# Scores and values of the first two key tiles ahead of the mean of x, and a new order of the first loads

## Chip, cores and metric

The kernel runs on one core of one Trainium2 chip. The metric is the device time of one execution in microseconds (us), the median of the runs.

## What is computed

Two layers on x of shape 8 x 64 x 64 x 64 (images, channels, rows, columns); n = 4096 positions. The first is attention with centred queries and keys plus a "unary" term, the second a binarised convolution with a gate. Only the first is touched by the change:

```python
xf = x.reshape(b, cin, n)
q = jnp.einsum('oc,bcn->bon', wq, xf) + bq[None, :, None]
k = jnp.einsum('oc,bcn->bon', wk, xf) + bk[None, :, None]
v = jnp.einsum('oc,bcn->bon', wv, xf) + bv[None, :, None]
q_mean = q.mean(axis=2, keepdims=True)
k_mean = k.mean(axis=2, keepdims=True)
q = q - q_mean
k = k - k_mean
sim = jnp.einsum('bcn,bcm->bnm', q, k) / (scale * TEMPERATURE)   # scale = 8
sim = jax.nn.softmax(sim, axis=2)
out = jnp.einsum('bnm,bcm->bcn', sim, v)
unary = jax.nn.softmax(jnp.einsum('bc,bcm->bm', q_mean[:, :, 0], k), axis=-1)
out_unary = jnp.einsum('bcm,bm->bc', v, unary)
out = out + out_unary[:, :, None]
return x + out.reshape(b, C, h, w)
```

## The kernel before

**Tiles.** Two images of 64 channels fill the 128 partitions: a "pair". There are 4 pairs, each with 8 blocks of 512 queries, and each block runs over 32 tiles of 128 keys. `projection()` (L157) forms mm = wq'wk once, so that scores come straight from x: for tile j, `scores` (L493) multiplies x's 128 key columns by q, where q = mm'x - mx, and mx is mm applied to the mean of x (`mean_scores`, L307, and `mean_scores_out`, L315). Four matmuls of 64 x 512 make the scores of one tile for both images (line L497), ScalarE takes exp with the scale 1/8 (L508), `weighted` (L511) multiplies by the values in four more matmuls (L516), and `summed` adds the exponentials for the denominator (L532, L534). `values(g)` (L329) makes the values of four key tiles at a time in 16 small matmuls with 65 columns: 64 of wv and one, mx + kb, whose exponential weights the unary term; kb = wk'bq comes from `key_bias()` (L162).

**Order.** Nothing is scheduled by a planner: `tc.manual_schedule()` keeps the order in which the program is written, engine by engine[...]. Waits come from the data: a tile that is written or read elsewhere is waited for as a whole, so that two engines that write two halves of one tile (q's halves in `queries_out`, L463) write one after the other. `attend` (L1079) runs over the 32 blocks; `plan(g)` lists, for each of the 32 key tiles of a block, what else is issued there with `put`. For each tile j it issues the scores of j, then the weighted product of j-1, then what the plan holds. In the first block, g = 0, the plan holds `values(i)` at tile 4i-1 (tile 0 for i = 0) and `unary_part(i)` at 4i+1, and at tile 0 `mix`, which makes the queries of block 1 in two matmuls (`pq`, L455) and their copies (L465 on VectorE, L466 on ScalarE).

**The start, which the change touches.** The loads are issued at L85 to L89: on ScalarE's queue wq, the second quarter of x, wv; on SyncE's queue wk and the three other quarters of x; on GpSimd's queue the 21 small vectors `vec`. Then (L1265 to L1286) TensorE gets 6 filler matmuls (`warm`, on a tile of ones; nothing reads the result), the projection, 4 fillers, the queries of block 0 without the mean (`queries`, L454), 18 fillers, the mean's matmul and the bias of keys; VectorE sums x's first and third quarter and half of the fourth (`mean_part`, L291), ScalarE the rest, between which lie `vectors()` (L167: three small VectorE operations on `vec`, a square root and a first exponential on ScalarE, each with a table load); `load_weights()` (L94) issues nine loads of convolution weights on SyncE after a VectorE memset; then `mean_sum`, `mean_scores`, `mean_scores_out`, `queries_out(0)` (the queries minus mx), `key_bias`, `value_weights` (L321), and the blocks begin.

Of the kernel before, what the change touches and what calls it, by code (L numbers as in the profile page):

```python
# [18 lines left out]
F32 = mybir.dt.float32  # L19
BF16 = mybir.dt.bfloat16  # L20
I32 = mybir.dt.int32
AF = mybir.ActivationFunctionType
ALU = mybir.AluOpType
# [3 lines left out]
P = 128  # L27
C = 64
# [3 lines left out]
QB = 512  # L32
NQ = N // QB
NK = N // P
ROWS = QB // HH
SPLIT = [slice(0, 224), slice(224, QB)]
H = C
# [8 lines left out]
def conv_seq_kernel(ctx, tc, x, wq, wk, wv, vecs, w1, w3, w5, wtap, gw, out):  # L46
    nc = tc.nc
    n_pairs = x.shape[0] * x.shape[1] // P
# [21 lines left out]
    def load_x(name, rows, queues=(nc.sync,)):  # L70
        xt = x_tile(name)
        for c in range(4):
            cols = bass.ts(c, N // 4)
            queues[c % len(queues)].dma_start(out=xt[:, cols], in_=xf[rows, cols])
        return xt
# [8 lines left out]
    w_tap = xp.tile([P, FIRST[3], C], F32, tag="v", name="w_tap")  # L84
    nc.scalar.dma_start(out=wq_s, in_=wq)  # L85
    nc.sync.dma_start(out=wk_s, in_=wk)
    nc.gpsimd.dma_start(out=vec, in_=vecs)
    xt = load_x("0", slice(0, P), (nc.sync, nc.scalar, nc.sync, nc.sync))
    nc.scalar.dma_start(out=wv_s, in_=wv)  # L89


# [56 lines left out]
    ngb = cp.tile([P, 1], F32, tag="ngb", name="ngb")  # L148
    inv = cp.tile([P, 3], F32, tag="inv", name="inv")

    def warm(n):

        t = ps_s.tile([P, 2, QB], F32, tag="s", name="warm")[:, 0, :]
        for _ in range(n):
            nc.tensor.matmul(t[:, 0:P], ones, ones, start=True, stop=True)  # L155

# [5 lines left out]
    def key_bias():  # L162
        t = m_tile("kb_p")
        nc.tensor.matmul(t[:, 0:1], wk_s, bq_s, start=True, stop=True)
        nc.vector.tensor_copy(kb, t[:, 0:1])  # L165

    def vectors():  # L167
        nc.vector.tensor_scalar(inv, rv, BN_EPS, None, ALU.add)
        nc.vector.tensor_scalar(bv2, bv_s, 2.0, None, ALU.mult)
        nc.vector.tensor_scalar(ngb, gb_s, -1.0, None, ALU.mult)  # L170
        nc.scalar.activation(inv, inv, AF.Sqrt)

        nc.scalar.activation(lim[:, 2:3], ones[:, 0:1], AF.Exp)
# [103 lines left out]
    class Pair:  # L277
# [40 lines left out]
            self.nmx = self.tile(sm, "nmx", 0, (P, 1))  # L318
            nc.vector.tensor_scalar(self.nmx, self.pm[:, 0:1], -1.0 / N, None, ALU.mult)

        def value_weights(self):  # L321

            self.v = self.tile(xp, "v", 0, (P, NK, P))
            wx = self.wx = self.tile(sm, "wx", 0, (P, C + 1))
            for b in range(2):
                nc.vector.tensor_copy(wx[img[b], 0:C], wv_s[img[b], img[b]])
            nc.vector.tensor_tensor(wx[:, C : C + 1], self.mx, kb, ALU.add)

        def values(self, g, unary=True):  # L329

            pv = ps_s.tile([P, 2, QB], F32, tag="s", name=f"pv_{self.name}_{g}")
            w = C + 1
            for i in range(4):
                for h in range(2):
                    for b in range(2):
                        nc.tensor.matmul(  # L336
                            pv[img[h], b, i * w : (i + 1) * w],
                            self.x[img[b], bass.ds((4 * g + i) * P + h * H, H)],
                            self.wx[img[b], :],
                            start=True,  # L340
                            stop=True,
                        )
            pvv = pv[:, :, 0 : 4 * w].rearrange("p b (t c) -> p b t c", c=w)
            nc.scalar.copy(
                self.v[:, 4 * g : 4 * g + 4, :].rearrange("p t (b c) -> p b t c", b=2),
                pvv[:, :, :, 0:C],
            )
            if unary:
                if g == 0:
                    self.eu = self.tile(sm, "eu", 0, (P, 2, NK))  # L350
                nc.scalar.activation(
                    self.eu[:, :, 4 * g : 4 * g + 4], pvv[:, :, :, C], AF.Exp
                )
# [136 lines left out]
            nc.vector.tensor_scalar(q[:, SPLIT[0]], data[0], self.mx, None, ALU.subtract)  # L490
            nc.scalar.activation(q[:, SPLIT[1]], data[1], AF.Identity, bias=self.nmx)

        def scores(self, qb, j, neg=None):  # L493
            ps = ps_s.tile([P, 2, QB], F32, tag="s", name=f"ps_{self.name}_{qb}_{j}")
            for h in range(2):
                for b in range(2):
                    nc.tensor.matmul(  # L497
                        ps[img[h], b, :],
                        self.x[img[b], bass.ds(j * P + h * H, H)],
                        self.q[qb][img[b], :],  # L500
                        start=True,
                        stop=neg is None,
                    )
            if neg is not None:
                for b in range(2):
                    nc.tensor.matmul(ps[:, b, :], ones[img[b], :], neg[img[b], :], start=False, stop=True)
            e = ep.tile([P, 2, QB], F32, tag="e", name=f"e_{self.name}_{qb}_{j}")
            nc.scalar.activation(e, ps, AF.Exp, scale=1.0 / 8.0)  # L508
            return e
# [559 lines left out]
    def acc_banks(name):  # L1069
        return [ps_a.tile([P, QB], F32, tag=f"acc{h}", name=f"{name}_{h}") for h in range(2)]  # L1070

    def misc_banks(name):
        return [m_tile(f"{name}_{h}") for h in range(2)]
# [2 lines left out]
    def rows_of(pr):  # L1076
        return slice(pr * P, (pr + 1) * P)

    def attend(pairs):  # L1079
        pending = None  # L1080
        n_blocks = n_pairs * NQ

# [6 lines left out]
        def plan(g):  # L1089
# [4 lines left out]
            def put(i, f, *a):  # L1094
                at.setdefault(i, []).append((f, a))
# [66 lines left out]
                    put((15, 12)[qb - 2] + 4 * i, pairs[pr - 1].store, NQ // 2 * (qb - 2) + i, rows_of(pr - 1))  # L1162
            if g == 0:
                for i in range(NQ):
                    put(max(4 * i - 1, 0), pairs[0].values, i)
                    put(4 * i + 1, pairs[0].unary_part, i)
                put(31, pairs[0].unary_sum)
                for i, n in enumerate((2, 1, 0)):
                    put(8 + 8 * i, weight_mean, n)
                    put(12 + 8 * i, weight_scale, n)  # L1170
# [38 lines left out]
        for g in range(n_blocks):  # L1209
            pr, qb = divmod(g, NQ)  # L1210
            at = plan(g)
            p = pairs[pr]
            for j in range(NK):
                new = (p, qb, j, p.scores(qb, j))
                if pending is not None:
                    pending[0].weighted(*pending[1:])
                    pending[0].summed(*pending[1:], g < n_blocks - 1)
                for f, a in at.pop(j, ()):
                    f(*a)
                pending = new  # L1220
            assert not at, at.keys()
# [42 lines left out]
    with tc.manual_schedule():  # L1264
        first = Pair("0", xt)  # L1265
        warm(6)
        projection()
        warm(4)
        first.mean_part(0, quarters[0])
        vectors()  # L1270
        first.mean_part(1, quarters[1], True)
        first.mean_part(2, quarters[2])
        for c in range(2):
            first.mean_part(3 + c, slice(N * (6 + c) // 8, N * (7 + c) // 8), c == 1)
        first.query_tiles(0, score_banks)
        for b in range(2):
            first.queries(0, b)
        load_weights()
        warm(18)
        first.mean_sum(5)  # L1280
        first.mean_scores()
        first.mean_scores_out()
        first.queries_out(0)
        key_bias()
        first.value_weights()
        attend([first] + [None] * (n_pairs - 1))  # L1286


    nb_ = sm.tile([P, 1], F32, tag="nb", name="nb")
# [127 lines left out]
```

## Time and profile before

| | |
|---|---|
| Three runs | 1902.95, 1903.20, 1903.52 us; median 1903.2 |
| Profiled execution, its own time | 1902.88 us |
| Its span, first to last instruction | 1901.1 us |
| TensorE busy / weight loads | 1882.2 us (99%) / 781.2 us (41%) |
| VectorE / ScalarE / GpSimd busy | 1587.3 us (83%) / 1276.6 us (67%) / 129.1 us (7%) |
| Mean granted TensorE clock | 0.997 |
| Scores, L497 | 8192 passes, 0.86 us for each tile's 8 when in full flow |
| First score matmul / first weighted product begin | 12.92 us / 17.15 us |

How to read it. The page gives one profiled execution; times within it count from its first instruction. PE is TensorE's matmuls, PEld its weight loads, DVE is VectorE, ACT ScalarE, POOL GpSimd, SP SyncE. One matmul in the program on 4-byte numbers stands as two in the profile (4 of a tile's scores are 8 there). Rows of the timeline are: start, length, engine, line, operation, what is written <- what is read, shape, count, and in brackets how long the engine stood idle before and what ended that. In tables of stages the columns are the stage, its length, busy time (and instructions) of PE, PEld, DVE, ACT and POOL, the granted TensorE clock, the share of the DMA engines and GB/s. The page names the releaser that came last by its own record; where two engines' results are waited for it can name a neighbour: the wait of ACT L466 is put down to the copy of kb, while the program has it wait for VectorE's half of q just before that.

### The profile page before, as it was taken

To read this page: it belongs to the slowest core of one execution; us is meant where nothing else is said; L and a number is where in the kernel's file an instruction comes from. 1 tells how busy PE (TensorE), PEld (TensorE's weight loads), DVE (VectorE), ACT (ScalarE), POOL (GpSimd) and SP (SyncE) were. 2 spreads that over 40 slices of the span, in tenths; PEclk is the share of its full clock that TensorE was granted. 3 is DMA by queue.
4 is the path that set the end of the run, shared out by engine and by line. 5 is a ranking of instruction groups with operands and counts; after the bars stand their busy time and mean duration, and the time that the engine had idled before them with its cause. 6 is when DMAs were issued, how large, how long until landed. Compare 5 with 4: busy or idle time off the path is not lost.

```text
span 1901.1 us, 50325 instructions
## 1 busy us (share of the span) xinstructions
PE 1882.2 (99%) x21502; PEld 781.2 (41%) x21502; DVE 1587.3 (83%) x2485; ACT 1276.6 (67%) x1639; POOL 129.1 (7%) x177
## 2 busy tenths in 40 slices
PE   9999999999999999999999999999999999999997
PEld 4333344443344434444434444434433344443343
DVE  6779888889888888888888888888887888887876
ACT  5666776666666676666666667666666666666663
POOL 0000000000000000000000000000000000000000
PEclk9999999999999999999999999999999999999998
DMA  4334433333333533333333444233333344333311
GB/s 124 65 60 102 80 68 72 67 58 72 67 71 82 122 81 82 65 72 66 58 71 68 102 112 92 51 79 67 70 67 64 65 84 94 85 72 63 71 35 47
DMA packets 73024, 142.22 MB, mean 75 GB/s; under 512 B 10380, under 2 KB 40920, under 8 KB 72664
## 3 DMA queue, kind: packets, MB, share of 16 engines
q0 software_dynamic: 22352, 81.29, 24.2%
q1 hardware_dynamic: 49720, 56.46, 10.4%
q8 instruction: 170, 2.79, 0.6%
q10 hardware_dynamic: 720, 1.18, 0.2%
q14 instruction: 62, 0.51, 0.1%
HBM read 39.27 MB, written 89.78 MB: 68 GB/s over the span
## 4 chain that ended last, share of the span: by engine, by line
PE 98%; DVE 1%; ACT 1%; DMA 0%; issue 0%; SPq 0%; DVEq 0%; ACTq 0%
PE ps L497 46%; PE acc L516 46%; PE z L804 2%; PE pv L336 1%; PE pq L483 1%; PE z L891 0%; PE z_5e L804 0%; DMA x<-in_x 0%; PE warm L155 0%; ACT e L508 0%; DVE r L609 0%; DVE sb L936 0%; ACT rc_ck L441 0%; DVE o L542 0%; DVE es_j L936 0%
## 5 line engine op out<-in xcount | busy, mean ns | idle before, releaser
L508 ACT ACTIVATE e<-ps 128x1024 f32<-128x1024 f32 x1024 | 1049.0, 1025 | 570.9 <-PE ps L497 557.9
L534 DVE TENSOR_TENSOR es<-es,e 128x1024 f32<-128x1024 f32 x836 | 1020.7, 1221 | 197.3 <-ACT e L508 184.0
L497 PE MATMUL ps<-q,x 64*64 64x512 f32 x8192 | 1084.5, 590 | 0.8 <-DVE kb L165 0.8
L516 PE MATMUL acc<-e,v 64*64 64x512 f32 x8192 | 1082.6, 589 | 2.2 <-ACT e L508 1.9
L516 PEld LDWEIGHTS acc<-e,v 64*64 64x64 f32 x8192 | 324.4, 131 | 558.7 <-ACT e L508 317.6
L497 PEld LDWEIGHTS ps<-q,x 64*64 64x64 f32 x8192 | 344.1, 133 | 493.5 <-issue 266.5
L555 POOL DMA_DIRECT2D es<-e x93 | 80.0, 860 | 902.1 <-ACT e L508 598.7
L871 DVE SCALAR_TENSOR_TENSOR sb<-pt,sb 128x256 f32<-128x256 f32 x174 | 65.9, 420 | 0.0
L804 PEld LDWEIGHTS <-wc 64*64 64x64 bf16 x3364 | 60.1, 106 | 2.7 <-issue 1.0
L555 POOL DMA_DIRECT2D es<-es x31 | 26.6, 857 | 440.3 <-DVE es L534 426.1
L804 PE MATMUL z<-ec,wc 64*64 64x128 bf16 x1392 | 53.6, 217 | 0.0
L532 DVE TENSOR_TENSOR es<-e,e 128x1024 f32<-128x1024 f32 x32 | 39.2, 1224 | 17.0 <-ACT e L508 17.0
L804 PE MATMUL z<-t,wc 64*64 64x128 bf16 x1392 | 53.1, 217 | 0.3 <-DVE o L542 0.3
L652 ACT ACTIVATE s<-x,vec 128x512 bf16<-128x512 f32 (+2 forms) x66 | 46.2, 702 | 7.7 <-DVE x L620 7.7
L834 ACT ACTIVATE pt<-z,frac 128x256 f32<-128x256 f32 (+1 forms) x87 | 41.1, 543 | 8.9 <-PE z L804 8.9
L839 DVE SCALAR_TENSOR_TENSOR pt<-z_5e,frac,pt 128x256 f32<-128x256 f32 x29 | 14.0, 484 | 38.2 <-PE z_5e L804 38.2
L553 POOL DMA_DIRECT2D es<-e x31 | 17.3, 558 | 339.6 <-ACT e L508 328.3
L542 DVE COPY o<-acc 128x512 f32<-128x512 f32 (+2 forms) x33 | 22.2, 675 | 9.6 <-PE acc L516 9.6
L845 DVE TENSOR_TENSOR pt<-pt 128x384 f32<-128x384 f32 x58 | 29.6, 552 | 0.0
L336 PEld LDWEIGHTS pv<-wx,x 64*64 64x64 f32 x1024 | 22.5, 134 | 16.9 <-issue 9.3
L570 DVE TENSOR_TENSOR e_parts<-e_parts 128x512 f32<-128x512 f32 x31 | 21.4, 689 | 6.3 <-DMA e_parts<-es 6.3
L620 DVE SCALAR_TENSOR_TENSOR x<-x,ou,x 128x512 f32<-128x512 f32 (+2 forms) x33 | 24.3, 736 | 1.2
(178 smaller groups left out, 882.6 us busy)
## 6 DMA issues: line engine op xcount, KB each, us to landing
es<-e POOLq DMA_DIRECT2D x124, 512.0 KB, 5.3
es<-es POOLq DMA_DIRECT2D x31, 512.0 KB, 5.4
e_parts<-es SPq DMA_DIRECT2D x124, 128.0 KB, 3.1
r<-rc SPq DMA_DIRECT2D x62, 128.0 KB, 3.0
out<-sb SPq DMA_DIRECT2D x28, 256.0 KB, 3.3
x<-in_x SPq DMA_DIRECT2D x24, 256.0 KB, 3.9
ec<-t SPq DMA_DIRECT2D x29, 99.0 KB, 4.7
xc<-in_x SPq DMA_DIRECT2D x30, 72.0 KB
```

Of the source, the lines that this page charges most:

```text
L336: nc.tensor.matmul(pv[img[h], b, i * w : (i + 1) * w], self.x[img[b], bass.ds((4 * g + i) * P + h * H, H)], self.wx[img[b], :], start=True ...
L497: nc.tensor.matmul(ps[img[h], b, :], self.x[img[b], bass.ds(j * P + h * H, H)], self.q[qb][img[b], :], start=True, stop=neg is None,)
L508: nc.scalar.activation(e, ps, AF.Exp, scale=1.0 / 8.0)
L516: nc.tensor.matmul(self.acc[qb][h][img[b], :], self.v[img[h], j, img[b]], e[img[h], b, :], start=(j == 0), stop=(j == NK - 1),)
L532: nc.vector.tensor_tensor(self.es[qb], self.first, e, ALU.add)
L534: nc.vector.tensor_tensor(self.es[qb], self.es[qb], e, ALU.add)
L555: nc.gpsimd.dma_start(out=out, in_=e, accum_op=ALU.add)
L652: nc.scalar.activation(sy[n][0][:, rows, pad : pad + HH], self.x2[qb][:, r0 * HH : r1 * HH].rearrange("p (h w) -> p h w", w=HH), AF.Sign, ...
L804: nc.tensor.matmul(z[img[b], :].rearrange("p (q w) -> p q w", w=HH), wc[k][img[h], n, c * C : c * C + C], src[:, first : first + step + 1 ...
L834: nc.scalar.activation(out, z, AF.Identity, scale=frac[:, by : by + 1])
L845: nc.vector.tensor_tensor(self.pairs[:, :, :, r, :], t[:, 0:3, 0], t[:, 0:3, 1], op)
L871: nc.vector.scalar_tensor_tensor(out, x, by, out, ALU.mult, ALU.add, **gap)
```

## The change

Three things are changed at the start of the program.

1. `vec` is loaded on ScalarE's queue, after the second quarter of x and before wv, and no longer on GpSimd's queue.
2. `vectors()` and `key_bias()` are issued before all of the sums of x, and `key_bias()` before the queries.
3. The queries of block 0 are copied as they are, without mx (`early_queries`). The scores of key tiles 0 and 1 are made from them, and the values of tiles 0 to 3 with 64 columns (`early_values`), before the sum of the second quarter of x. When mx is known, `early_columns` makes two columns more, in 16 matmuls with 2 columns: x times (mx + kb), the unary exponent, and x times -mx/8, which is what the mean takes off the scores. `early_exponentials` gives the latter to ScalarE as the bias of the exponential, for each image by itself (four instructions of 512 columns in place of two of 1024). `mean_to_queries` then takes mx from q for all of the later tiles. Of the 18 fillers ahead of the mean's matmul 2 are left, now after the second tile's scores. `values(0)` no longer stands in the plan of the first block.

What is computed stays the same. The diff:

```diff
--- before.py
+++ after.py
@@ -84,8 +84,8 @@
     w_tap = xp.tile([P, FIRST[3], C], F32, tag="v", name="w_tap")
     nc.scalar.dma_start(out=wq_s, in_=wq)
     nc.sync.dma_start(out=wk_s, in_=wk)
-    nc.gpsimd.dma_start(out=vec, in_=vecs)
     xt = load_x("0", slice(0, P), (nc.sync, nc.scalar, nc.sync, nc.sync))
+    nc.scalar.dma_start(out=vec, in_=vecs)
     nc.scalar.dma_start(out=wv_s, in_=wv)
 
 
@@ -148,9 +148,9 @@
     ngb = cp.tile([P, 1], F32, tag="ngb", name="ngb")
     inv = cp.tile([P, 3], F32, tag="inv", name="inv")
 
-    def warm(n):
-
-        t = ps_s.tile([P, 2, QB], F32, tag="s", name="warm")[:, 0, :]
+    def warm(n, one=None):
+
+        t = one("warm") if one else ps_s.tile([P, 2, QB], F32, tag="s", name="warm")[:, 0, :]
         for _ in range(n):
             nc.tensor.matmul(t[:, 0:P], ones, ones, start=True, stop=True)
 
@@ -318,13 +318,80 @@
             self.nmx = self.tile(sm, "nmx", 0, (P, 1))
             nc.vector.tensor_scalar(self.nmx, self.pm[:, 0:1], -1.0 / N, None, ALU.mult)
 
-        def value_weights(self):
-
+        def value_tiles(self):
             self.v = self.tile(xp, "v", 0, (P, NK, P))
-            wx = self.wx = self.tile(sm, "wx", 0, (P, C + 1))
+            wx = self.wx = self.tile(sm, "wx", 0, (P, C + 2))
             for b in range(2):
                 nc.vector.tensor_copy(wx[img[b], 0:C], wv_s[img[b], img[b]])
-            nc.vector.tensor_tensor(wx[:, C : C + 1], self.mx, kb, ALU.add)
+
+        def value_weights(self, tiles=True):
+
+            if tiles:
+                self.value_tiles()
+            nc.vector.tensor_tensor(self.wx[:, C : C + 1], self.mx, kb, ALU.add)
+
+
+        def early_queries(self, qb):
+
+            q = self.q[qb] = self.tile(sm, "q", qb)
+            nc.vector.tensor_copy(q[img[0]], self.pq[0][img[0]])
+            nc.scalar.copy(q[img[1]], self.pq[1][img[1]])
+
+        def early_values(self):
+
+            pv = self.pv = acc_banks(f"pv_{self.name}_e")
+            for i in range(4):
+                for h in range(2):
+                    for b in range(2):
+                        nc.tensor.matmul(
+                            pv[b][img[h], i * C : (i + 1) * C],
+                            self.x[img[b], bass.ds(i * P + h * H, H)],
+                            self.wx[img[b], 0:C],
+                            start=True,
+                            stop=True,
+                        )
+
+        def early_values_out(self):
+            for b in range(2):
+                nc.scalar.copy(
+                    self.v[:, 0:4, img[b]], self.pv[b][:, 0 : 4 * C].rearrange("p (t c) -> p t c", c=C)
+                )
+
+        def early_columns(self):
+
+            nc.vector.tensor_scalar(self.wx[:, C + 1 : C + 2], self.nmx, 1.0 / 8.0, None, ALU.mult)
+            pb = misc_banks(f"pb_{self.name}_e")
+            for i in range(4):
+                for h in range(2):
+                    for b in range(2):
+                        nc.tensor.matmul(
+                            pb[b][img[h], 2 * i : 2 * i + 2],
+                            self.x[img[b], bass.ds(i * P + h * H, H)],
+                            self.wx[img[b], C : C + 2],
+                            start=True,
+                            stop=True,
+                        )
+            self.add = self.tile(sm, "add", 0, (P, 2, 4, 2))
+            for b in range(2):
+                nc.vector.tensor_copy(
+                    self.add[:, b], pb[b][:, 0:8].rearrange("p (t c) -> p t c", c=2)
+                )
+
+        def early_exponentials(self, ps, j):
+            e = ep.tile([P, 2, QB], F32, tag="e", name=f"e_{self.name}_e{j}")
+            for b in range(2):
+                nc.scalar.activation(
+                    e[:, b, :], ps[:, b, :], AF.Exp, scale=1.0 / 8.0, bias=self.add[:, b, j, 1:2]
+                )
+            return e
+
+        def early_unary(self):
+            self.eu = self.tile(sm, "eu", 0, (P, 2, NK))
+            nc.scalar.activation(self.eu[:, :, 0:4], self.add[:, :, :, 0], AF.Exp)
+
+        def mean_to_queries(self, qb):
+            q = self.q[qb]
+            nc.vector.tensor_scalar(q, q, self.mx, None, ALU.subtract)
 
         def values(self, g, unary=True):
 
@@ -336,7 +403,7 @@
                         nc.tensor.matmul(
                             pv[img[h], b, i * w : (i + 1) * w],
                             self.x[img[b], bass.ds((4 * g + i) * P + h * H, H)],
-                            self.wx[img[b], :],
+                            self.wx[img[b], 0:w],
                             start=True,
                             stop=True,
                         )
@@ -490,7 +557,7 @@
             nc.vector.tensor_scalar(q[:, SPLIT[0]], data[0], self.mx, None, ALU.subtract)
             nc.scalar.activation(q[:, SPLIT[1]], data[1], AF.Identity, bias=self.nmx)
 
-        def scores(self, qb, j, neg=None):
+        def scores(self, qb, j, neg=None, exp=True):
             ps = ps_s.tile([P, 2, QB], F32, tag="s", name=f"ps_{self.name}_{qb}_{j}")
             for h in range(2):
                 for b in range(2):
@@ -504,6 +571,8 @@
             if neg is not None:
                 for b in range(2):
                     nc.tensor.matmul(ps[:, b, :], ones[img[b], :], neg[img[b], :], start=False, stop=True)
+            if not exp:
+                return ps
             e = ep.tile([P, 2, QB], F32, tag="e", name=f"e_{self.name}_{qb}_{j}")
             nc.scalar.activation(e, ps, AF.Exp, scale=1.0 / 8.0)
             return e
@@ -1076,7 +1145,7 @@
     def rows_of(pr):
         return slice(pr * P, (pr + 1) * P)
 
-    def attend(pairs):
+    def attend(pairs, early):
         pending = None
         n_blocks = n_pairs * NQ
 
@@ -1162,7 +1231,8 @@
                     put((15, 12)[qb - 2] + 4 * i, pairs[pr - 1].store, NQ // 2 * (qb - 2) + i, rows_of(pr - 1))
             if g == 0:
                 for i in range(NQ):
-                    put(max(4 * i - 1, 0), pairs[0].values, i)
+                    if i > 0:
+                        put(4 * i - 1, pairs[0].values, i)
                     put(4 * i + 1, pairs[0].unary_part, i)
                 put(31, pairs[0].unary_sum)
                 for i, n in enumerate((2, 1, 0)):
@@ -1211,7 +1281,7 @@
             at = plan(g)
             p = pairs[pr]
             for j in range(NK):
-                new = (p, qb, j, p.scores(qb, j))
+                new = (p, qb, j, early[j] if g == 0 and j < len(early) else p.scores(qb, j))
                 if pending is not None:
                     pending[0].weighted(*pending[1:])
                     pending[0].summed(*pending[1:], g < n_blocks - 1)
@@ -1266,24 +1336,33 @@
         warm(6)
         projection()
         warm(4)
+        vectors()
+        key_bias()
         first.mean_part(0, quarters[0])
-        vectors()
+        first.query_tiles(0, score_banks)
+        for b in range(2):
+            first.queries(0, b)
+        first.early_queries(0)
+        first.value_tiles()
+        early = [first.scores(0, 0, exp=False)]
+        first.early_values()
+        early.append(first.scores(0, 1, exp=False))
         first.mean_part(1, quarters[1], True)
         first.mean_part(2, quarters[2])
         for c in range(2):
             first.mean_part(3 + c, slice(N * (6 + c) // 8, N * (7 + c) // 8), c == 1)
-        first.query_tiles(0, score_banks)
-        for b in range(2):
-            first.queries(0, b)
         load_weights()
-        warm(18)
+        warm(2, m_tile)
         first.mean_sum(5)
         first.mean_scores()
         first.mean_scores_out()
-        first.queries_out(0)
-        key_bias()
-        first.value_weights()
-        attend([first] + [None] * (n_pairs - 1))
+        first.early_values_out()
+        first.value_weights(False)
+        first.early_columns()
+        early = [first.early_exponentials(ps, j) for j, ps in enumerate(early)]
+        first.early_unary()
+        first.mean_to_queries(0)
+        attend([first] + [None] * (n_pairs - 1), early)
 
 
     nb_ = sm.tile([P, 1], F32, tag="nb", name="nb")
```

`acc_banks` and `misc_banks` each give two banks of PSUM; the first pair is also what the weighted products of a block use, the second what the queries of the next block use.

## Prediction

> **What bounds the kernel now.** I read the page's first part, the chain of waits, then the chain and the timeline of the first 20 us, where everything that the change touches lies.
>
> ```profile
> PE 1882.2 (99%) x21502; PEld 781.2 (41%) x21502; DVE 1587.3 (83%) x2485; ACT 1276.6 (67%) x1639; POOL 129.1 (7%) x177
> ```
>
> TensorE (PE) is busy 99% of the span and carries 98% of the chain. From 17.15 us on it alternates four score matmuls (0.86 us) and four weighted ones (0.86 us) almost without a hole. So the change can only move the moment at which this alternation begins, and the whole kernel follows by that amount. The chain up to there (start, length, what):
>
> ```profile
> 1.20 4.96 DMA x<-in_x
> ...
> 7.37 4.21 PE warm L155 x36
> 11.58 0.23 PE pm L311 x4
> ...
> 12.07 0.71 DVE q L465
> ...
> 14.75 1.02 ACT e L508
> 15.80 0.68 ACT q L466
> ...
> 16.51 0.59 ACT v L344
> ...
> 17.15 1.09 PE acc L516 x8
> 18.24 0.86 PE ps L497 x8
> ```
>
> The reader is to see a serial ladder: mean of x (pm), queries (q), scores, exponentials (e), values (v), first weighted product (acc). Inside it 4.2 us of filler (warm), behind which the mean's matmul stands. The timeline tells what the filler covers (start, length, engine, line, operation, instructions):
>
> ```profile
> 1.06 2.93 PE L155 MATMUL warm<-ones 128*128 128x128 f32 x12 [1.06 <-DVE lim L122]
> ...
> 6.29 1.08 PE L455 MATMUL pq<-x,mm 64*64 64x512 f32 x4 [0.36 <-DMA x<-in_x]
> 7.30 4.29 PE L155 MATMUL warm<-ones 128*128 128x128 f32 x36
> ...
> 6.18 1.22 DVE L301 TENSOR_REDUCE xs<-x 128x1 f32<-128x1024 f32 x1 [1.43 <-DMA x<-in_x]
> 7.32 0.16 DVE L168 TENSOR_SCALAR inv<-vec 128x3 f32<-128x3 f32 x1
> ...
> 8.77 1.99 DVE L301 TENSOR_REDUCE xs<-x 128x1 f32<-128x1024 f32 x2 [1.18 <-DMA x<-in_x]
> ...
> 10.90 0.16 DVE L305 TENSOR_REDUCE xm<-xs 128x1 f32<-128x5 f32 x1
> ```
>
> The mean is ready at 11.06 and cannot come much earlier: the trace's completion events put the last quarter of x at 10.05. The filler delays it by 0.45 us more. The two filler rows also show the clock: 12 pieces in 2.93 us (0.24 each), later 36 in 4.29 (0.12 each). The trace's clock record grants full speed from 5.6 us.
>
> [...] Between 5.9 and 7.5 us, when wv follows the second quarter of x on ACT's ring (q10) while SP's ring (q1) brings x:
>
> ```profile
> q1 hardware_dynamic: 134, 0.50, 85.9%
> q10 hardware_dynamic: 127, 0.08, 16.4%
> ```
>
> (packets, MB, share.) About one small packet goes per 4 KB packet of x, so the 64 KB of wv took as long as 0.5 MB: issued at 1.67, complete at 8.95. [...]
>
> ```profile
> 1886.34:1889.75 3.41, 1.52 (x8) 1.01 (x9) 2.50 (x10) 0.26 (x1) 0.00 (x0) 1.00 0.00 0
> 1889.76:1893.17 3.41, 1.95 (x3) 0.34 (x1) 2.98 (x5) 1.17 (x2) 0.00 (x0) 0.50 0.70 247
> ```
>
> A window with PE 45% busy (1.52 of 3.41) was followed by clock 0.50[...]. The least busy full-size window that kept the clock was 52% busy (from 162.6). So a window need not be quite idle here.
>
> **The change part by part.** All against the profiled execution: 1902.88 us, span 1901.1; the median of the runs is 0.3 above it.
>
> *vec behind x on ACT's ring.* It takes the place that wv has now, with packets of 84 instead of 512 bytes. The turns with x cost it about the same, so I take completion at 8.6; the bounds are 7.3 (no turns taken, or where the POOL queue brings it now: 7.25) and 8.95 (wv now). wv then lands near 10, x unchanged. POOL loses a 0.7 us issue; ACT gains one of 0.45 ahead of its first table load, which then ends near 3.9, long before its first use at 8.8.
>
> *vectors() and key_bias() first.* VectorE (DVE) now waits for vec before it touches x, and PE before the queries, which today start at 6.29. Behind DVE's wait stand all of its reductions of x; behind PE's, everything. After 8.6: three small operations 0.27, PE's kb_p 0.38 in parallel, the copy 0.14 at 9.15 to 9.3, then the reduction of the first quarter (1.2) to 10.5. This is a new cost of 3.1 us on DVE against 7.40 now. ACT's square root and second table load (1.28) end at 10.6, ahead of need.
>
> *Queries without the mean.* PE's queries end at 10.1 at full clock. The copy of one half (0.67, as L542's copy) ends at 11.15, ACT's copy of the other half (0.6, it waits for the first since both write one tile) at 11.85. ACT's two parts of the mean follow (1.04 + 0.61 + 0.19), DVE's wx copies 0.33, and quarters 1.2 + 0.7: xm at 13.9 instead of 11.06.
>
> *Work moved ahead of the mean on PE.* After 11.85: rest of the first scores 0.65, values 0.47, second scores 0.86, two filler matmuls 0.47, so pm starts at 14.35. PE, not xm, is last by 0.45. Saved behind it: scores, values and their copies lie before the mean now, as do 16 of the 18 filler matmuls.
>
> *The bias path.* From pm: 0.28 for the matmul, 0.05 to mx, 0.36 for nmx and two columns of wx, 16 tiny matmuls, not in the trace. I price them as the 16 of L336 (0.47)[...]. Two DVE copies of 8 columns 0.26: the bias is ready at 16.0. Exponentials of 512 columns with a bias pointer: the row L466 gives 0.68 for one[...]. First half at 16.65, second at 17.25. The weighted product follows half by half (2 x 0.43) to 17.85. The mean's subtraction from q [...] hides under the exponentials; without that cover it would delay the third scores by its length.
>
> *Sum.* The scores of the third tile start at 17.85 instead of 18.06 (PE's timeline): 0.2 us gained at full clock. The next three exponentials and q of block 1 end before PE wants them (e of tile 2 at 19.7, wanted at 20.4), so nothing is given back. load_weights() moves 3 us later with its nine DMAs on SP; w5 lands at 20.6 now and is first read at 30.46. The xc loads behind them are 40 us early.
>
> *The clock.* PE now stops at 5.93 and has nothing until 8.7. In the window 5.6 to 9.01 it would be some 20% busy, below the 45% that dropped the clock at the end. I take it that the clock halves from 9.01 to 12.43. The queries then end at 10.8, q 0.4 later, and a part of the first scores runs slow: together 0.5 us more. Net 0.3 slower, 1902.88 + 0.3 + 0.3 to the median = 1903.5.
>
> **The rivals.**
> 1. *The clock stays up* (windows lie otherwise, or 20% is enough): 0.2 gained, **1903.0**.
> 2. *vec lands early*, 7.3 to 7.8, because ACT's ring isn't held up by turns. For it: 15 of the 16 parts of wv were complete by 8.73, most at 7.9. The ladder shifts by as much: 1.5 to 0.3 gained with either clock, say **1902.2**.
> 3. *The slower side: the clock is down for two windows*, 9.01 to 15.84. [...] first scores, values, second scores and filler (2.45 us) then cost up to twice that and stand in front of pm, which starts at 16.5 instead of 14.8. All later steps shift: 2.0 slower than now, **1905.2**. It decides if the window 9.01 to 12.43, some 70% busy, isn't enough to raise the clock. Against it: at the start one full window was enough.
> 4. *The whole path is missed*: if the exponentials of tile 2 ran late behind ACT's new queue (four halves, eu, q), PE would wait about 0.3: within the forecast's range.
>
> **How the numbers follow.** Forecast 0.42, rival 1 0.2, rival 2 0.17, rival 3 0.18, rest 0.03. The range 1901.9 to 1905.3 leaves out the early end of rival 2 and the far end of rival 3, with vec at 8.95. About 0.2% (3.8 us) is what a measurement of this kernel can tell from no change. No case reaches it: x at 10.05 forbids starting 3.8 us earlier, and later would need vec at some 10.5 and two slow windows. So same 0.95, faster 0.02, slower 0.03.
>
> **What would show it.** In the changed profile: kb_p and the vec operations start near 8.6 and queries behind them; PE idle from 5.9 to there; a clock of 0.50 near 9 to 12.4, or rows of queries twice as long; pm released by PE's own queue, not by xm; the third scores near 18.4. A vec completion before 8 or pm before 14 would make me wrong to the fast side, pm after 16 to the slow side.

## The result, and the profile after

| | before | after |
|---|---|---|
| Median of 15 runs each (lowest to highest) | 1903.20 us (1902.24 to 1903.96) | 1907.14 us (1905.58 to 1908.53) |
| Profiled execution, its own time / its span | 1902.88 / 1901.1 us | 1907.15 / 1905.4 us |

The ratio is 1.0020 (95% interval 1.0013 to 1.0027): 3.9 us slower, just beyond the 3.8 us that the prediction set for a difference, and 3.6 us above its number. In these 15 runs the changed kernel spreads further (3.0 us) than the kernel before (1.7 us). That alone is no mark of the change: among the 49 runs of the kernel before that stand beside e1 to e4, nine form a second group at 1904.67 to 1905.76.

The first part of the page of the changed kernel:

```profile
PE 1882.8 (99%) x21502; PEld 782.5 (41%) x21502; DVE 1587.6 (83%) x2489; ACT 1277.2 (67%) x1642; POOL 128.9 (7%) x176
```

TensorE's busy time hardly moved (1882.2 before): as forecast, only the start can matter. The chain of waits of the first 22 us (start, length, what):

```profile
1.68 6.69 DMA vec<-in_vecs
...
8.41 0.59 PE kb_p L164 x2
8.99 1.92 PE pq L522 x4
...
10.94 0.69 DVE q L337
...
11.68 2.07 PE ps L564 x6
13.75 1.05 PE pv_e L346 x22
...
15.12 1.71 PE ps L564 x7
16.83 0.96 PE warm L155 x4
17.79 0.23 PE pm L311 x4
...
18.61 0.70 PE pb_e L367 x32
```

Where the old chain had x, then filler, then the mean's matmul at 11.58, the new one has vec, queries, scores, values, scores, and the mean's matmul at 17.79. The timeline of the same kernel (start, length, engine, line, operation, count, idle before) tells why so late:

```profile
4.21 1.92 PE L155 MATMUL warm<-ones 128*128 128x128 f32 x8
8.41 0.59 PE L164 MATMUL kb_p<-vec,wk_s 128*128 128x1 f32 x2 [2.28 <-DMA vec<-in_vecs]
8.92 1.97 PE L522 MATMUL pq<-x,mm 64*64 64x512 f32 x4
11.68 2.59 PE L564 MATMUL ps<-q,x 64*64 64x512 f32 x8 [0.78 <-DVE q L337]
...
14.05 0.16 DVE L305 TENSOR_REDUCE xm<-xs 128x1 f32<-128x5 f32 x1 [0.26 <-ACT mean L294]
18.05 0.16 DVE L317 TENSOR_SCALAR mx<-pm 128x1 f32<-128x1 f32 x1 [3.83 <-PE pm L311]
...
19.50 2.42 ACT L383 ACTIVATE e_e<-ps,add 128x512 f32<-128x512 f32 x4 [3.69 <-DVE add L376]
...
22.79 1.03 ACT L577 ACTIVATE e<-ps 128x1024 f32<-128x1024 f32 x1
```

The last row, the exponential of tile 2, is in the kernel before:

```profile
19.16 1.02 ACT L508 ACTIVATE e<-ps 128x1024 f32<-128x1024 f32 x1 [1.07 <-PE ps L497]
```

The same four query matmuls took 1.08 us before and 1.97 now; the first scores 2.59. In this execution TensorE runs at half clock all the way from its first matmul: the trace's clock record grants full speed only from 17.47 us (before: from 5.60). In e2, e3 and e4 below the clock changes of one trace stood 3.41 us apart, or twice that: 17.00 and 20.42 (e2), 9.77 and 16.60 (e3), 7.38, 14.21 and 17.62 (e4). The stretch of full clock is 1884.157 us long before and 1880.744 here, which differ by 3.41. A clock window, below, is a stretch of 3.41 us counted from a change of its own trace. Other executions had other patterns: their mean granted clock is 0.994 to 0.996, against 0.998 here, where the stretch ahead of the first record isn't counted as slow. The mean was ready at 14.21, and VectorE then stood 3.83 us for pm. The exponential of tile 2 begins 3.63 us later than before. This shift stays the same to about 920 us, then two stalls add 0.3 and 0.42, at about 926 and 1146 us. With them the sum is 4.3, the difference of the spans.

The second stall stands behind transfers es<-e to DRAM and changes from execution to execution (0.42 here, 0.2 in e9 below, none in e5). The first does not. It lies between two exponentials of ScalarE, here in the changed kernel and then in the kernel before:

```profile
929.87 1.03 ACT L577 ACTIVATE e<-ps 128x1024 f32<-128x1024 f32 x1 [1.03 <-PE ps L564]
```

```profile
925.97 1.02 ACT L508 ACTIVATE e<-ps 128x1024 f32<-128x1024 f32 x1 [0.74 <-PE ps L497]
```

All seven traces of programs with 1642 ScalarE instructions (the changed kernel, e1, e2, e4, e5, e6, e9) have this stall, 0.3 us at the same exponential. None of the six others has it there (1639 in the kernel before and e3, 1641 in e7, e8 and e10, 1643 in e11). The chain of waits shows no transfer at that place, only 0.34 us in which ScalarE waits for nothing that the profile shows. So the stall belongs to the program and not to one execution; its cause is open.

### The profile page after: what moved, and what is told of

Same layout as the page of the kernel before. It is cut to its first block, busy times and chain, and to the rows that moved or that the text cites. A ratio compares the mean times of both kernels' runs of the same rounds, so it can differ in the third digit from the quotient of the medians.

```text
span 1905.4 us, 50330 instructions
## 1 busy us (share of the span) xinstructions
PE 1882.8 (99%) x21502; PEld 782.5 (41%) x21502; DVE 1587.6 (83%) x2489; ACT 1277.2 (67%) x1642; POOL 128.9 (7%) x176
## 4 chain that ended last, share of the span: by engine, by line
PE 96%; DMA 1%; DVE 1%; ACT 1%; issue 0%; ACTq 0%; SPq 0%; DVEq 0%
PE ps L564 46%; PE acc L585 45%; PE z L873 2%; PE pv L403 1%; PE pq L550 1%; PE z L960 0%; PE z_5e L873 0%; DMA es<-e 0%; ACT e L577 0%; DMA vec<-in_vecs 0%; DMA es<-es 0%; DVE r L678 0%; PE pq L522 0%; DMA e_parts<-es 0%; DVE es L603 0%
```

## The experiments

**Theory.** In the new order TensorE stops twice (6.1 to 8.4 for vec, 10.9 to 11.7 for q), so no clock window before 14.05 is full (65% to 80% busy), and the half clock delays everything. **Rivals**: vec's late arrival itself; ScalarE's new queue; the new order as such. Each ratio below is to runs of the kernel before taken beside the experiment (medians 1902.90 to 1903.21); it isn't the plain quotient of two medians.

**e1: fill the first stop.** From the changed kernel, nothing reads the fillers' results:

```diff
         projection()
-        warm(4)
+        warm(13)
         vectors()
```

> The changed kernel with 13 filler matmuls instead of 4 after the projection, so that TensorE is busy until the small vectors are there. Clock theory (TensorE's stop from 6.1 to 8.4 us kept the clock at half until 17.5, which doubled the matmuls ahead of the mean's): full clock from some 5 to 8 us on, queries about 1.0 us long instead of 1.97, the mean's matmul near 14.3 instead of 17.7, time 1903.0 to 1903.8. Order theory (the wait for vec and the queue of work ahead of the mean's matmul cost the time whatever the clock): no gain, 1906.5 to 1907.5.

Measured: 1905.47 us (1903.28 to 1907.75), ratio 1.0011 (1.0004 to 1.0017). The profiled execution had the full clock from 5.29 on and took 1903.92. Its timeline:

```profile
8.70 1.08 PE L522 MATMUL pq<-x,mm 64*64 64x512 f32 x4
...
14.32 0.28 PE L311 MATMUL pm<-xm,mm 64*64 64x1 f32 x4
...
17.75 0.72 PE L564 MATMUL ps<-q,x 64*64 64x512 f32 x2
17.89 0.60 PE L585 MATMUL acc<-e_e,v 64*64 64x512 f32 x2
```

pm at 14.32 instead of 17.72: in this pair of executions half clock cost 3.4 us. So the clock is the larger part of the shift. But the median misses what was expected (1903.0 to 1903.8): most of the 21 runs lie well above the profiled one. The mean granted clock of the runs goes along with that: it is 0.997 or 0.998 in the eight runs up to 1904.71, and 0.995 or 0.996 in the nine from 1906.20 on. So the slower ones had half clock for longer. Two stops remain in the profile, 0.96 us ahead of the first scores and 0.61 after the mean's matmul.

**e2: fill the second stop too.**

```diff
-        warm(4)
+        warm(13)
...
             first.queries(0, b)
+        warm(4, m_tile)
         first.early_queries(0)
```

> As the fill of the first stop, and 4 fillers more between the queries and the first scores, where TensorE waits for the copies of q. Clock theory: if the second stop still loses the clock in some executions, this is faster and steadier than the fill of the first stop alone (1902.8 to 1903.4, spread under 1 us); if one filled stop is enough, the two are equal. Order theory: 1906.5 to 1907.5.

Measured: 1904.26 us (1903.33 to 1906.43), ratio 1.0006 (0.9998 to 1.0014). This is faster and steadier than e1, as the clock theory asks, but outside its 1902.8 to 1903.4. In the profiled execution a window now fell on the third stop, around the mean's tiny matmuls. The table of stages cut at this trace's clock windows (stage, length, busy time of PE, PEld, DVE, ACT, POOL, clock, DMA share, GB/s):

```profile
10.18:13.59 3.41, 3.41 (x56) 1.96 (x55) 2.96 (x8) 2.91 (x9) 0.00 (x0) 1.00 0.02 5
13.59:17.00 3.41, 2.54 (x48) 1.56 (x44) 1.05 (x7) 1.06 (x4) 0.00 (x0) 1.00 0.33 87
17.00:20.42 3.42, 3.42 (x19) 2.77 (x20) 2.32 (x3) 2.49 (x5) 0.00 (x0) 0.50 1.02 247
```

TensorE was 74% busy (2.54 of 3.41), and the clock fell to 0.50 for the next window.

**e3: the kernel before without its fillers.** A cross-check from the other side:

```diff
         load_weights()
-        warm(18)
         first.mean_sum(5)
```

> The kernel before without its 18 fillers ahead of the mean's matmul, nothing else. Clock theory: TensorE stops from 7.4 to 11.1 us, the clock is at half when the scores begin, and the kernel gets slower by 1 to 3 us although the mean's matmul comes 0.45 us earlier: 1904.2 to 1906.2. Order theory (fillers only delay): faster by 0.4, 1902.8.

Measured: 1904.46 us (1903.63 to 1905.37), ratio 1.0008 (0.9999 to 1.0016), within what the clock theory expected. pm came 0.23 earlier (11.28), but the clock was down from 9.77 to 16.60 and a tile's eight score passes took 2.67 us. The 18 fillers, which look like a delay of 0.45 us in the chain, thus save about 1.2 us by the medians (the interval just includes none).

**e4: vec on GpSimd's queue again**, ahead of x, with everything else as changed:

```diff
+    nc.gpsimd.dma_start(out=vec, in_=vecs)
     xt = load_x("0", slice(0, P), (nc.sync, nc.scalar, nc.sync, nc.sync))
-    nc.scalar.dma_start(out=vec, in_=vecs)
```

> The changed kernel with the small vectors on GpSimd's queue again, issued ahead of x as before the change (complete at 7.25 us then, at 8.37 now). Wait-for-vec theory: all of the start comes 1.1 us earlier, 1906.0. Clock theory: 1.1 us from the wait, and the clock comes up in more of the executions since TensorE's stop is half as long: 1904.5 to 1906.0 with a spread of 2 us or more.

Measured: 1903.13 us, ratio 1.0003 (0.9995 to 1.0011). The median is below what either theory expected. The runs make two groups: seven from 1901.72 to 1903.13, six from 1904.64 to 1905.81. The profiled execution is of the second. Its stages, cut at its clock windows:

```profile
3.97:7.38 3.41, 1.76 (x15) 1.49 (x15) 0.73 (x6) 0.39 (x2) 0.13 (x1) 1.00 0.97 350
7.38:10.79 3.41, 2.63 (x9) 0.81 (x9) 2.94 (x6) 2.43 (x4) 0.00 (x0) 0.50 0.42 166
10.79:14.21 3.42, 3.42 (x47) 1.78 (x40) 1.14 (x4) 1.86 (x6) 0.00 (x0) 0.50 0.05 10
14.21:17.62 3.41, 2.54 (x48) 1.56 (x44) 1.05 (x7) 0.70 (x2) 0.00 (x0) 1.00 0.90 227
17.62:21.03 3.41, 3.41 (x19) 2.75 (x20) 2.30 (x3) 2.50 (x5) 0.00 (x0) 0.50 1.00 223
```

In these rows the clock goes with the busy time of the row above. After 52% busy it falls, after 77% it stays down, after 100% it rises, and after 74% it falls again. That the place of the windows against the stops decides between the lower and the upper group is argued, not shown: no run of the lower group was profiled, and the mean clocks of the groups overlap (0.996 to 0.998 and 0.995 to 0.997). But it is one program in two groups, so the order of the work alone can't make the difference between them.

**e5: fill every stop.** As e2, and around the tiny matmuls:

```diff
         first.value_weights(False)
+        warm(2, acc_one)
         first.early_columns()
+        warm(2, acc_one)
```

(`acc_one` gives one bank of `acc_banks`.)

> The changed kernel with all three stops of TensorE filled: 13 fillers for 4 while vec is awaited, 4 between queries and scores, 2 and 2 around the small matmuls of the bias. Clock theory: the clock stays up in nearly all executions, so the cost of the clock is gone and what is left is the change at full clock with the late vec: 1903.2 to 1903.8, spread under 1.5 us. If the clock were only a part: 1904.5 or more with a spread like that of the two fills before.

Measured: 1904.13 us, ratio 1.0003 (0.9995 to 1.0011), somewhat above the expected 1903.2 to 1903.8, and the spread shrank to 1903.58 to 1905.27. With the stops filled the changed kernel gains 3.0 us on itself. The profiled execution has the full clock from 3.97:

```profile
14.34 0.28 PE L311 MATMUL pm<-xm,mm 64*64 64x1 f32 x4
...
19.42 1.02 ACT L577 ACTIVATE e<-ps 128x1024 f32<-128x1024 f32 x1
```

Its exponentials run 0.26 us behind those of the kernel before. That is small, but not the 0.2 ahead that the forecast has at full clock. Two questions are left: what vec's place costs, and where the 0.2 went.

**e6: as e5, with vec on GpSimd's queue** (the edit of e4) and `warm(7)` in place of `warm(13)`, since the first stop is shorter.

> The same fills (7 in the first stop, which is shorter) with the small vectors on GpSimd's queue. Clock theory with the wait for vec as a separate term: 1.2 us below the filled kernel with vec behind x, 1902.0 to 1902.6, spread under 1.5 us, without the slow half (1904.6 to 1905.8) that the unfilled kernel with vec on GpSimd's queue has. If vec's place works only through the clock: equal to the filled kernel with vec behind x, 1903.5.

Measured: 1902.17 us (1901.27 to 1903.23), ratio 0.9992 (0.9983 to 1.0000), as expected.

```profile
6.63 0.17 DVE L168 TENSOR_SCALAR inv<-vec 128x3 f32<-128x3 f32 x1 [1.88 <-DMA vec<-in_vecs]
...
12.67 0.28 PE L311 MATMUL pm<-xm,mm 64*64 64x1 f32 x4
```

vec is there at 6.63 instead of 8.38, pm comes at 12.67 instead of 14.34, and the median falls by 2.0. So vec behind x costs about 2 us, even when the clock costs nothing. In the six traces with vec on ScalarE's queue its first reader starts at 8.36, 8.38, 8.39, 8.56, 8.83 and 9.49 us: the arrival itself varies by 1.1.

**e7: nothing waits for vec.** The pieces of the change that serve, without those that cost: vec on GpSimd's queue, queries ahead of vectors and the bias of keys, both halves of q copied by VectorE, the copies of wv by GpSimd, scores of both tiles ahead of the values, no filler ahead of the mean. The core of the edit, from the changed kernel:

```diff
-        vectors()
-        key_bias()
         first.mean_part(0, quarters[0])
...
             first.queries(0, b)
+        vectors()
+        kb_t = key_bias()
         first.early_queries(0)
+        key_bias_out(kb_t)
+        first.mean_part(1, quarters[1], True)
         first.value_tiles()
-        early = [first.scores(0, 0, exp=False)]
+        early = [first.scores(0, 0, exp=False), first.scores(0, 1, exp=False)]
         first.early_values()
...
-        warm(2, m_tile)
```

> The changed kernel with vec on GpSimd's queue and without the second part of the change: queries and the first sum of x ahead of vectors and key bias, both halves of q copied by VectorE so that ScalarE's table load is not in the way, wv's copies on GpSimd, no fillers ahead of the mean's matmul and none added. Order theory: scores and values lie in the shadow of x's loads, the mean's matmul comes near 11.3 us, third scores near 14.9 instead of 18.06, at full clock 1900.0. Clock theory: TensorE stops from 7.8 to 9.0 and from 11.6 to 13.8, so some executions lose the clock: median 1900.5 to 1902.5, spread 2 us or more.

Measured: 1899.97 us (1899.43 to 1905.71), ratio 0.9986 (0.9979 to 0.9992): faster than both kernels, by 3.2 us than the one before. Its timeline:

```profile
6.52 1.08 PE L525 MATMUL pq<-x,mm 64*64 64x512 f32 x4 [0.39 <-DMA x<-in_x]
7.52 0.38 PE L164 MATMUL kb_p<-vec,wk_s 128*128 128x1 f32 x2
8.46 2.24 PE L567 MATMUL ps<-q,x 64*64 64x512 f32 x13 [0.55 <-DVE q L340]
...
11.43 0.22 PE L314 MATMUL pm<-xm,mm 64*64 64x1 f32 x3
```

The queries wait for x alone, the real work stands where the filler stood before, and the mean's matmul is at 11.4, where it was in the kernel before, but with scores and values behind it already. So in this order scores and values ahead of the mean are worth about 3 us, with the filler gone and the copies on other engines. From the changed kernel to e7 the median falls by 7.2 us: 3.0 go with the filled stops (e5), 2.0 with vec's queue (e6), and the 2.2 from e6 to e7 with the other pieces of e7, which no run separates.

**e8: e7 with fillers in its stops**, five behind the bias of keys and two on each side of the tiny matmuls.

> The same with fillers in TensorE's stops: 5 between the bias of keys and the first scores, 2 and 2 around the small matmuls of the bias. Both theories together: 1900.0 to 1900.8, spread under 1.5 us, faster than both kernels. If the bias path itself eats the gain: 1902.5 or more.

Measured: 1900.28 us (1899.71 to 1903.05), ratio 0.9987 (0.9979 to 0.9995). The quickest execution is 0.3 later and tile 2's exponential of the profile 0.5 (16.90 against 16.39); the median is no better. The range is narrower only by e7's one run at 1905.71: three of 13 runs lie above 1902 here, three of 21 in e7. In this start, whose stops are short, fillers brought nothing that these runs show.

**e9: ScalarE's queue.** In e5 ScalarE works four early exponentials, eu, its half of the queries of block 1, and only then, with no idle time, the exponential of tile 2. My first explanation of the lost 0.4 was this queue. From e5, with the queries of block 1 two tiles later:

```diff
-            put(0, both)
+            put(2 if g == 0 else 0, both)
```

> As e5_fill_all, but the queries of block 1 are made at key tile 2 instead of 0, so that ScalarE's 0.68 us copy of them no longer stands between the four early exponentials and the exponential of tile 2. Theory (ScalarE's queue gives back what the new order gained): the exponential of tile 2 starts near 18.7 instead of 19.42, that of tile 3 near 20.7 instead of 21.13, and the steady shift against the kernel before falls from +0.23 to about -0.2; median near 1903.7, 0.4 below e5_fill_all (1904.13). Rival (TensorE's own order of passes sets the start of tile 3's exponential): tile 2's exponential moves, tile 3's stays at 21.1 and the median stays at 1904.1.

Measured: 1905.17 us, ratio 1.0011 (1.0004 to 1.0017), 1.0 slower than e5. vec came 0.44 later in the profiled execution; with that taken off, the exponential of tile 2 starts at 19.42, exactly as in e5, although ScalarE now idles 0.78 us ahead of it, waiting for scores:

```profile
19.86 1.02 ACT L577 ACTIVATE e<-ps 128x1024 f32<-128x1024 f32 x1 [0.78 <-PE ps L564]
```

The theory fell: the queue was no bound. That the copy moved behind tile 2 costs another 0.85 there (tile 3's exponential at 22.43) is a plain loss.

**e10: the same edit on e7.**

> As e7_x_first, with the queries of block 1 at key tile 2 instead of 0. Theory (ScalarE's queue): the exponential of tile 2 starts near 15.65 instead of 16.39, the shift against the kernel before grows from -2.77 to about -3.2 and the best times fall from 1899.5 to about 1899.1, median near 1899.6. Rival (TensorE's order of passes, or a clock lost more often as TensorE has two matmuls less between the tiny ones and the weighted product): no change, or a median above 1900.

Measured: 1902.22 us (1900.15 to 1905.70), ratio 0.9996 (0.9988 to 1.0005), against 1899.97 for e7. Without the two query matmuls TensorE stands 1.0 us ahead of the first weighted product, and in the profiled execution the clock then fell: four score passes from 15.22 on took 1.35 us, 0.74 in e7.

**e11: the first weighted product waits for both halves.** In e5's timeline the passes of score and weighted matmuls no longer come in groups of 8, but by ones, threes and fours, mixed. The first weighted product starts when the exponential of the first image is ready, 0.6 us ahead of the other's; I now suspected that one image's passes run ahead and the other's lag. So from e5, a copy of one number onto itself, behind the second half:

```diff
                     e[:, b, :], ps[:, b, :], AF.Exp, scale=1.0 / 8.0, bias=self.add[:, b, j, 1:2]
                 )
+            if j == 0:
+                nc.scalar.copy(e[:, 0, 0:1], e[:, 0, 0:1])
             return e
```

> As e5_fill_all, with one number of tile 0's first half copied onto itself by ScalarE after the exponential of its second half, so that the first weighted product starts with both halves ready, some 0.8 us after the first half. Theory (the half-by-half start puts the passes of the two images out of step and gains nothing): rows of 8 passes again in the weighted products and scores, tile 3's exponential about 0.15 later than in e5_fill_all, steady shift about +0.4 against +0.23, median near 1904.3. Rival (the half-by-half start is a real gain of a half): everything from the first weighted product on moves by 0.5 to 0.8, steady shift +0.8 to +1.0, median near 1904.8.

Measured: 1904.40 us, ratio 1.0004 (0.9996 to 1.0012). First e5's timeline, then that of e11:

```profile
15.23 0.64 PE L367 MATMUL pb_e<-wx,x 64*64 64x2 f32 x32
...
17.34 0.74 PE L585 MATMUL acc<-e_e,v 64*64 64x512 f32 x4
17.77 0.59 PE L564 MATMUL ps<-q,x 64*64 64x512 f32 x1
17.79 0.73 PE L585 MATMUL acc<-e_e,v 64*64 64x512 f32 x3
18.20 0.74 PE L564 MATMUL ps<-q,x 64*64 64x512 f32 x4
...
22.21 1.09 PE L564 MATMUL ps<-q,x 64*64 64x512 f32 x8
```

```profile
16.34 0.64 PE L367 MATMUL pb_e<-wx,x 64*64 64x2 f32 x32
...
18.63 1.09 PE L587 MATMUL acc<-e_e,v 64*64 64x512 f32 x8
19.54 1.04 PE L566 MATMUL ps<-q,x 64*64 64x512 f32 x8
...
23.43 1.09 PE L566 MATMUL ps<-q,x 64*64 64x512 f32 x8
```

e11's whole ladder is 1.11 later, as vec came later (pb_e 16.34 against 15.23). Counted from pb_e, the first weighted product starts 0.66 later than in e5 (2.29 against 1.63, where e5's first pass starts at 16.86), but the scores of tile 4 only 0.11 later (7.09 against 6.98), and the rows are in groups of 8 again. So nearly all of the half-by-half start is given back: it gains 0.11, not the 0.6 that a half is early (the 0.66 and the 0.11 both hold the copy itself, which ends 0.07 us after the second half).

## Why the prediction was wrong

**What failed: "The clock".** The forecast took the clock's rise at 5.6 us from the one profile of before, let it fall from 9.01 to 12.43 only, and asked 0.5 us for it. In the changed kernel's profile there was no rise until 17.47, and that cost 3.4 us (pm at 17.72; at full clock 14.32 and 14.34 in e1 and e5). By the medians, filling the stops took back 3.0 us (e5). The prediction's own sign for the slow side, pm after 16, came true. Two readings were wrong in this step. First, the windows do not lie at the same place: the first clock change of the traces is at 3.97 us (e4, e5), 5.29 (e1), 5.60 (before), 6.41 (e6), 6.76 (e2) or 17.47 (after). In the kernel before TensorE works from 1.06 to 12.1 us with one stop of 0.36 us, so that any window inside that stretch is at least 89% busy ((3.41 - 0.36) / 3.41), wherever it lies. The new one stops at 6.1 and at 10.9, and four windows of its profile in a row were not full (the first begins ahead of the first matmul at 1.06):

| Window | TensorE busy | Clock after it |
|---|---|---|
| 0.40 to 3.81 | 2.75 us, 80% | half |
| 3.81 to 7.23 | 2.32 us, 68% | half |
| 7.23 to 10.64 | 2.23 us, 65% | half |
| 10.64 to 14.05 | 2.63 us, 77% | half |
| 14.05 to 17.47 | 3.42 us, 100% | full |

Second, the prediction's rival 3 had this mechanism ("the clock is down for two windows", 1905.2, chance 0.18), with the point from which it decides put rightly: that some 70% busy isn't enough to raise the clock (in the table 65% to 80% were not). Its counterargument, that "at the start one full window was enough", assumed the full window (before, 2.18 to 5.60: 100% busy). And the clock could be down from the beginning, for 17 us instead of 7: the rival and the range were too small by 2 us. The sentence that no case reaches 3.8 us fell with it: 3.9 was reached with vec at 8.37, and not at "some 10.5".

The forecast put the new kernel's windows where the one profile had them, 5.60 and steps of 3.41 us from there; that was an assumption of the author's, and the changes listed above stand elsewhere. Its line between the 45% busy that dropped the clock and the 52% that kept it didn't hold either: the clock fell here after windows that were 74% (e2, e4) and 52% (e4) busy.

**What failed second: "The bias path" and "Sum".** "The weighted product follows half by half (2 x 0.43) to 17.85", "nothing is given back". (The terms themselves end at 17.68: the second half at 17.25 and one 0.43.) At full clock the first pass of the third scores was at 17.75 and 17.77 (e1, e5), forecast 17.85. But this was one image's passes running ahead, and the start of a row isn't that of a tile: counted by later tiles, the kernel is 0.26 behind the one before instead of 0.2 ahead. The place named for the risk in rival 4, ScalarE's queue, was wrong (e9). What e11 shows is the size: the half-by-half start, booked in full, gains 0.11. That it is lost because the next exponential waits for both images' scores, while one image's passes run ahead, is how I read the two timelines. By e1's records, two score passes of the third tile (17.75) start ahead of the last two passes of the first weighted product (17.89), which the program issues first.

**A size that was off: "vec behind x on ACT's ring".** It landed at 8.37 in the profile (forecast 8.6, bounds 7.3 and 8.95). That number held, but over executions it reaches 9.49, outside the bounds, and no rival asked what the old queue would have given in the new order: 6.63, about 2.0 us of the median (e5 and e6).

**What held.** Durations and places: TensorE idle from 6.1 to vec; kb's copy at 9.03 (forecast 9.15); half of q 0.68 (0.67); xm at 14.21 in the profile; PE, not xm, last ahead of pm; pm at full clock 14.32 to 14.34 (14.35), though by luck; exponentials of a half 0.605 each (2.42 for four; the forecast's two end 0.60 apart, an estimate of the author's); the tiny matmuls 0.64 (the forecast's 16.0 for the bias has 0.77 for them: 0.47 as in L336 and 0.3 by the author's estimate), with 2 columns as long as those with 65 in the kernel before (0.65 at 21.49); q's subtraction 0.48, under the exponentials. load_weights() and the xc loads show no cost, as the shift is the same from 22 to 920 us. The luck in pm: at full clock xm was ready at 13.27 and 13.29 (e1, e5; forecast 13.9) and the second half of q at 11.29 and 11.31 (11.85), both early, but TensorE needed 3.0 us from there to pm and not 2.5. Two errors of half a microsecond cancelled.

**The sum with measured terms.** Half clock 3.4 and the start at full clock +0.26 make 3.66, against the 3.63 of the profile. The stall at 926 us adds 0.3, which makes 3.96, and the medians differ by 3.94. That fit is partly luck, since the half clock of one execution stands in it for that of all. In e5 the same two terms, 0.26 and 0.3, are over half of the 1.0 us by which its median lies above the kernel before. In its profile the end adds 0.3 more: there the clock fell 13.8 us ahead of the last instruction, in the kernel before 11.4. Over the 13 traces the stretch from the last exponential to the end takes 29.8 to 31.1 us. Whether the clock makes this difference too was not tried.

## What to carry to other kernels

A filler on TensorE isn't only a delay: the 18 of the kernel before save about 1.2 us by the medians (e3). Ask for each stop how busy the clock window around it becomes, wherever the windows may lie (the first change of these traces stands anywhere from 3.97 to 17.47 us), and not only where the profile shows them. Before a small load is put ahead of everything, ask which queue brings it (2.0 us by the medians of e5 and e6) and who stands behind it; e7 keeps the early scores, drops the wait, and is 3.2 us faster than the kernel before. When a stall seems an accident of one execution, look for it in the traces of the other variants: the one at 926 us came back seven times. A stage that starts on half of its data need not gain the time of that half: here it gained 0.11 of 0.6 us (e11).

## What the runs showed of the hardware

- The clock rose after windows of 3.41 us that were busy for 85% (e4: 0.55 to 3.96; e5: 0.56 to 3.97) and for 100% (before: 2.18 to 5.60; after: 14.05 to 17.47; e4: 10.79 to 14.21), and once for 78% (e10, at its end, 1889.15 to 1892.56). It did not after 80% (after) or 77% (after, e4).
- It fell after windows busy for 31% (e3, 6.36 to 9.77), 52% and 74% (e4). It stayed up after 46% (after, 1887.97 to 1891.39), 52% (before, 162.61 to 166.02), 60% (e10, 5.00 to 8.41), 70% (e5, 7.39 to 10.80), 72% (e1, 8.70 to 12.11), 74% (after, 17.47 to 20.88) and 78% (e7, 9.64 to 13.05). So between 46% and 74% the busy share of the records alone doesn't tell whether the clock fell, nor between 77% and 80% whether it rose; what else decides was not tried.
- A load of 10.5 KB issued at 1.68 on ScalarE's queue behind a quarter of x took 6.69 us to land; on GpSimd's queue its first reader started at 6.63 and 6.79 (e6, e4).
- In e5, where the first exponentials of the two images end 0.6 us apart, the score and weighted passes from 16.86 to 20.50 come by ones, threes, fours and sevens, mixed, and by eights at 20.50, 22.21 and 23.12. In e11, where the first weighted product waits for both, they come by eights from 18.63 on.
